# A decoder layer with an interleaved schedule: side work placed by an account of the engines' time, other context products, one conversion on ScalarE, y's split earlier, LayerNorm's buffers locked apart

## The chip, the cores and the metric

The program runs on one core of a Trainium2 chip. The metric is the time of one execution on the device in microseconds (us). TensorE (PE in the profile) multiplies matrices and loads weights beside it (PEld); VectorE (DVE), ScalarE (ACT) and GpSimd (POOL) work element by element; SyncE (SP) issues DMAs, and so does POOL. Each engine runs its own list of instructions in order and waits on semaphores for the others.

## The reference, cut to what matters

A batch of 16 sequences of 256 tokens of width 512 goes through one decoder layer: x plus a Mamba-2 mixer, plus a linear cross attention on a context, plus a gated feed-forward network (FFN) with quantised weights and activations.

```python
x = x + _L0_attn_ref(_layernorm(x), ...)                       # Mamba-2, 32 heads of 64, state 64
x = x + _L0_xattn_ref(_layernorm(x), ctx_1024, ctx_1024, ...)  # 16 heads of 32
x = x + _L0_ffn_ref(_layernorm(x), w_gate, w_up, w_down)       # 2048 inner, weights to -1, 0, 1

# _L0_xattn_ref
qh = sigmoid(q @ wq + bq); kh = sigmoid(k @ wk + bk)
vh = (v @ wv + bv).reshape(b, s, h, dv)
kv = einsum('bsh,bshd->bhd', kh, vh)
state = cumsum(kv, axis=1)
out = einsum('bsh,bhd->bshd', qh, state).reshape(b, s, d) @ wo + bo
```

## The kernel before, in words

**Pairs, slots and units.** Two batches make a pair (k = 0 to 7). The 2048 inner channels of the mixer are cut into 16 units of 128. One unit of one pair is a slot: 128 slots, one after the other, in the loop at line 1927. A slot s works on three units in flight: u0 = s is projected, u1 = s-1 is scanned out and u2 = s-2 goes through the output product. On TensorE a slot is always: six of the 12 products of the z projection (L676), the four transposes of u1's x (`turn_x`, L941), the other six, the 12 products of the x projection (L676, `project_part(u0, 1)`), u1's scan output (`scan_out`, L961 and L968), and u2's output product (L1011, 12 products into four accumulators that stand for a whole pair).

**The other engines in a slot.** VectorE: `times_g` (L929, L933), `scan` (two of L912), then the three convolution taps of u0 (L693, which read the x projection in PSUM after `conv_x`, L897), `plus_dx` (L976) and `gated` (L981), which makes y. ScalarE: eight of L951 (`x_dt`), `silu_z` (L891), the copy yh of y (L987, in `split_y`), `conv_x` (L897), the square of y (L998), `cross` (four of L920) and `silu_x` (L906). POOL: yl = y - yh (L988) and the sum of squares (L999). yh and yl are y's two halves for the output product; each has one buffer, and so has y.

**Side work.** Everything else is written as Python generators that yield what they need next ("dve, 0.7 us"), and `advance(now)` lets them go on at eight points of a slot. POINTS = 8; VectorE's steps may stand at points 1, 2, 5 and 6, ScalarE's at 0, 5 and 6, TensorE's at 3 (just before the scan output, in a turn of the two projection banks, called "z") and at 7 (after the output product, in a bank of its own). What may stand there is decided by `due` (line 1714) from a sum per engine and half slot that has a ceiling (`room`, 2.0 to 4.0 us), and by `Banks.take` (line 297) for PSUM. A step marked "must" (`leaves`) is placed whatever the sum. The side work is: the next pair's LayerNorm (`norm_transposed`, line 607), its time steps (`time_steps`, line 698) and states (`states`, line 777), all started by `plan` three slots before the end of a pair (`c == NU - 3`, for the pair after the next); the end of a batch with its attention queries (`batch_end`, line 1049); the context, two batches at a time (`context_pair`, line 1201), and its groups (`context_group`, line 1298); and the quantising of the FFN's weights (`ffn_quantised`, line 1463) in 48 chunks.

**The FFN** follows in 32 tiles of 128 tokens, 48 products of 128 x 512 each (L1579, L1621).

**Order.** The program's order is written out by hand (`manual_schedule`), so an engine's list is exactly the order in which the Python text calls. A DMA on SP or POOL that waits for data holds up those behind it.

**Locks of the generators.** `Shared` counts a resource in the order of the text. `lns` (one) stands for the normalised tile y ("ln") and its two 16-bit halves ("ln_hi", "ln_lo") together and is held from the load to the transposing DMAs; `turned` (two) for the transposed halves of a pair; `attends` (one) for the attention's tail; `chunks` (three) for weight chunks.

Of the kernel before, what the change touches and what calls it, by code (L numbers as in the profile page):

```python
# [36 lines left out]
F32 = mybir.dt.float32  # L37
# [10 lines left out]
P = 128  # L48
# [10 lines left out]
def decoder_kernel(  # L59
# [135 lines left out]
    with ExitStack() as part:  # L195
# [74 lines left out]

        class Shared:
# [16 lines left out]
        class Banks:  # L288
# [3 lines left out]
            def __init__(self):  # L292
                self.free = {"own": True, "z": True}
                self.line = []
                self.since = 0

            def take(self, own=False, first=False):
                me = [own]
                self.line.insert(0 if first else len(self.line), me)
                while True:  # L300
                    moment = clock[0] % POINTS
                    if steady() and moment == 3:

                        others = [one for one in self.line if not one[0]]
                        if self.free["z"] and others and others[0] is me:
                            hold = "z"
                            break
                    elif self.free["own"] and self.line[0] is me and (
                        not steady() or moment == 7 and clock[0] >= self.since
# [5 lines left out]
                self.free[hold] = False  # L315
                return hold

            def give(self, hold):
                self.free[hold] = True
                if hold == "own":  # L320
                    self.since = clock[0] + 4

        bank = Banks()

        def misc(hold, shape, name):
# [5 lines left out]
        chunks, stages, lns, turned, turned_q, attends, ctxs, outs, xs, late, preps, streams = (  # L331
            Shared(n) for n in (3, 3, 1, 2, 1, 1, 1, 2, 3, 1, 2, 2)
# [274 lines left out]
        def norm_transposed(src, b, what, store):  # L607

            yield from lns.take(rank=0 if what == "m" else 2 if "late" in store else 1)
# [13 lines left out]
            nc.vector.tensor_scalar(rs, mv[:, :, 1], EPS, LN_UP**-2, ALU.add, ALU.mult)  # L623
            hi = p1.tile([P, NT, D], F16, tag="ln_hi", name=f"lnh_{what}_{b}")
# [13 lines left out]
            nc.gpsimd.tensor_tensor(lo, y, hi, ALU.subtract)  # L638
            if what == "q":
                yield from turned_q.take(rank=2 if "late" in store else 1)  # L640
# [14 lines left out]
            lns.give()  # L655
# [42 lines left out]
        def time_steps(pair):  # L698
# [4 lines left out]
            hold = yield from bank.take(first=True)  # L703
# [49 lines left out]
            hold = (yield from bank.take(first=True)) if k else "tp"  # L753
# [23 lines left out]
        def states(pair):  # L777
# [5 lines left out]
            hold = yield from bank.take()  # L783
# [26 lines left out]
            for j in range(2):  # L810
                yield pe(0.4)
                hold = yield from bank.take()
                pg = misc(hold, [P, 3, P], f"pg_{k}_{j}")
                for n, (s0, t0) in enumerate(((0, 0), (P, P), (0, P))):
                    nc.tensor.matmul(
                        pg[:, n, :], bcT[0:NS, j, s0 : s0 + P], cT[:, j, t0 : t0 + P],
                        start=True, stop=True,
# [3 lines left out]
                    g[:, j, 0:2, :], pg[:, 0:2, :], upper.unsqueeze(1).to_broadcast([P, 2, P]),  # L821
# [1265 lines left out]
```

## Time and profile before

| | |
|---|---|
| median of 3 runs | 1882.19 us (1882.07 to 1885.43) |
| the profiled execution, its own time | 1887.88 us |
| its span, first to last instruction | 1886.1 us |
| busy in the span: PE, DVE, ACT, POOL | 95%, 87%, 66%, 36% |
| first slot's scan output to the end of pair 0 | 50.5 to 242.5 us |
| pairs 1 to 7, scan output to scan output | 242.5 to 1525.8 us |
| the rest, FFN above all | 1525.8 to 1886.1 us |

A busy TensorE is not one at its peak, since matmuls are pipelined: the products of 128 x 512 last 383 ns each by their rows but start 0.215 us apart. What counts is the stretch from one slot's start to the next. An engine that is not the last to arrive may idle at no cost.

### The profile page before, as it was taken

The page shows a single profiled execution, that of the slowest core. Times are in us where ns is not written, and L with a number is a line of the kernel's source. Part 1 is how long each engine was busy: PE and PEld are TensorE (multiplying, and loading weights), DVE is VectorE, ACT ScalarE, POOL GpSimd, SP SyncE. Part 2 cuts the span into 40 slices and gives each one's busy share as a digit, 9 for nine tenths or more (in the row PEclk, how much of TensorE's full clock was granted, in tenths as well). Part 3 has the DMA queues.
Part 4 walks back from the last instruction along what each step waited for, and adds up shares of the span by engine and source line. Part 5 has one row for each costly group of instructions (what it writes and reads, how often), then busy time and mean ns, then how long its engine had stood idle before and what let it go on. Part 6 is the DMA issues. An engine that isn't in the chain of part 4 may idle for free.

```text
span 1886.1 us, 30373 instructions
## 1 busy us (share of the span) xinstructions
PE 1786.5 (95%) x10464; PEld 1018.1 (54%) x10464; DVE 1638.2 (87%) x2711; ACT 1248.1 (66%) x2896; POOL 682.2 (36%) x691
## 2 busy tenths in 40 slices
PE   6789999998999998999999999998999989999998
PEld 4445555555556555555555555565656544444443
DVE  6989888777888889888988998989887888999997
ACT  5777666675666666666666666666666557777775
POOL 1233432344434354546454636463533222211000
PEclk8999999999999999999999999999999999999999
DMA  5764776788768777877597879787867734655454
GB/s 163 240 185 136 235 191 174 217 257 223 168 196 270 201 196 235 258 192 191 185 268 211 199 205 252 202 193 186 238 188 213 250 89 99 133 123 130 108 120 95
DMA packets 296933, 358.95 MB, mean 190 GB/s; under 512 B 163765, under 2 KB 197861, under 8 KB 296778
## 3 DMA queue, kind: packets, MB, share of 16 engines
q1 hardware_dynamic: 277962, 296.13, 60.0%
q0 software_dynamic: 18240, 60.84, 9.4%
q8 instruction: 83, 1.36, 0.3%
q14 instruction: 72, 0.59, 0.1%
q10 hardware_dynamic: 576, 0.04, 0.0%
HBM read 279.70 MB, written 39.58 MB: 169 GB/s over the span
## 4 chain that ended last, share of the span: by engine, by line
PE 57%; DVE 25%; DMA 7%; ACT 5%; issue 4%; POOL 2%; SPq 1%; ACTq 0%; POOLq 0%; DVEq 0%
PE pp L676 21%; PE po L1011 11%; PE po_f L1621 5%; PE pg L1579 4%; PE pu L1579 4%; DVE m L912 4%; DVE xs L693 4%; PE py L961 4%; DVE m L929 2%; PE trx L941 2%; DMA w<-w_d 2%; PE py L968 2%; DVE m L933 1%; DVE sp_q L742 1%; DVE y L976 1%
## 5 line engine op out<-in xcount | busy, mean ns | idle before, releaser
L676 PE MATMUL pp<-lnT_h_m,w 128*128 128x512 f16 (+1 forms) x2056 | 661.1, 383 | 23.3 <-DVE xs L693 20.8
L676 PEld LDWEIGHTS <-w 128*128 128x128 f16 x3084 | 296.5, 99 | 364.3 <-issue 35.8
L988 POOL TENSOR_TENSOR yl<-y,yh 128x512 fp32r<-128x512 f32 x128 | 178.9, 1398 | 717.5 <-ACT yh L987 659.3
L693 DVE SCALAR_TENSOR_TENSOR xs<-pp,convw_sb,xs 128x510 f32<-128x510 f32 (+2 forms) x384 | 286.1, 745 | 151.1 <-ACT xs L897 141.6
L676 PE MATMUL pp<-lnT_l_m,w 128*128 128x512 f16 (+1 forms) x1028 | 393.4, 383 | 0.0
L1011 PE MATMUL po<-wout,yh 128*128 128x512 f32 x1024 | 337.0, 410 | 4.6 <-DMA wout<-wout_d 4.6
L951 ACT ACTIVATE xdt<-trx,dt 128x64 f32<-128x64 f32 x1024 | 223.5, 328 | 167.4 <-PE trx L941 167.3
L912 DVE TENSOR_TENSOR_SCAN m<-dab,starts 128x512 f32<-128x512 f32 x254 | 302.2, 1230 | 0.5 <-DMA dab<-da_d 0.5
L1011 PEld LDWEIGHTS po<-wout,yh 128*128 128x128 f32 x1024 | 183.8, 189 | 61.3 <-issue 15.1
L1011 PE MATMUL po<-wout,yl 128*128 128x512 f32 x512 | 203.7, 398 | 3.0 <-POOL yl L988 3.0
L906 ACT ACTIVATE xs<-xs 128x512 f32<-128x512 f32 x128 | 80.9, 632 | 186.3 <-DVE xs L693 186.3
L961 PE MATMUL py<-m,xdt 128*64 128x256 f32 x1024 | 162.1, 395 | 11.1 <-DVE m L933 5.2
L1579 PEld LDWEIGHTS <-yT 128*128 128x128 bf16 x1024 | 100.0, 98 | 131.1 <-issue 14.7
L920 ACT ACTIVATE m<-edb,m 128x128 f32<-128x128 f32 x508 | 162.7, 395 | 12.1 <-DVE m L912 12.1
L999 POOL TENSOR_TENSOR ssq<-ssq,sq 128x512 f32<-128x512 f32 x120 | 158.6, 1321 | 27.9 <-ACT sq L998 27.0
L897 ACT ACTIVATE xs<-pp,convb_sb,convw_sb 128x512 f32<-128x512 f32 x128 | 100.3, 783 | 102.2 <-PE pp L676 102.1
L929 DVE TENSOR_TENSOR m<-m,g 128x1024 f32<-128x1024 f32 x128 | 161.9, 1265 | 0.1
L1579 PE MATMUL pg<-w_ffn,yT 128*128 128x512 bf16 x512 | 132.3, 381 | 4.7 <-ACT h L1583 4.7
L1579 PE MATMUL pu<-w_ffn,yT 128*128 128x512 bf16 x512 | 132.3, 381 | 4.6 <-DVE x L1037 4.6
L1621 PE MATMUL po_f<-w_ffn,hT 128*128 128x512 bf16 x512 | 125.4, 379 | 2.0 <-DMA hT<-hq 2.0
L1583 ACT ACTIVATE h<-pg,sg 128x512 f32<-128x512 f32 x128 | 86.6, 683 | 51.6 <-PE pg L1579 51.3
L1011 PEld LDWEIGHTS po<-wout,yl 128*128 128x128 f32 x512 | 96.7, 189 | 29.7 <-POOL yl L988 6.4
(278 smaller groups left out, 2791.9 us busy)
## 6 DMA issues: line engine op xcount, KB each, us to landing
dab<-da_d SPq DMA_DIRECT2D x127, 512.0 KB
wout<-wout_d SPq DMA_DIRECT2D x112, 512.0 KB
edb<-ed_d SPq DMA_DIRECT2D x127, 256.0 KB
w<-w_d SPq DMA_DIRECT2D x40, 512.0 KB
raw<-in_w_zx SPq DMA_DIRECT2D x16, 512.0 KB
wout_d<-wout SPq DMA_DIRECT2D x16, 512.0 KB
ctxT<-in_ctx_t POOLq DMA_DIRECT2D x16, 512.0 KB, 7.8
x<-in_x SPq DMA_DIRECT2D x16, 512.0 KB
```

Source lines behind the costliest of these rows:

```text
L676: nc.tensor.matmul(dst, w(wi, kc), yT[yi][:, :, kc, :], start=n == 0, stop=n == 3 * KD - 1)
L693: nc.vector.scalar_tensor_tensor(u[:, :, d:S], raw[:, :, 0 : S - d], w[:, j : j + 1], u[:, :, d:S], ALU.mult, ALU.add,)
L912: nc.vector.tensor_tensor_scan(u["m"][:, 4 * j : 4 * j + 4, :].rearrange("p k t -> p (k t)"), u["da"][j].rearrange("p h i t -> p (h i t)") ...
L920: nc.scalar.activation(u["m"][:, 8 + n, :], u["ed"][:, n // 2, n % 2, :], AF.Copy, scale=u["m"][:, 2 * n, P - 1 : P],)
L929: nc.vector.tensor_tensor(m, m, gi.unsqueeze(2).to_broadcast([P, 2, 2, NT * P]), ALU.mult)
L951: nc.scalar.activation(u["xdt"][:, j, i, h, :], u["tr"][:, j, i, h * HD : (h + 1) * HD], AF.Copy, scale=dt[:, i, j, 2 * c + h : 2 * c + h ...
L961: nc.tensor.matmul(py[h * HD : (h + 1) * HD, j, :].rearrange("p (i t) -> p i t", i=NT), xdt[:, j, 0, h, :], m[:, 2 * (2 * j + h) : 9 + 2 * ...
L988: nc.gpsimd.tensor_tensor(lo, u["y"], hi, ALU.subtract)
L999: nc.gpsimd.tensor_tensor(pair["ssq"], pair["ssq"], sq, ALU.add)
L1011: nc.tensor.matmul(pair["po"][n], u["yhl"][yi][:, j, i * P : (i + 1) * P], w[:, wi, :], start=c == 0 and p == 0, stop=c == NU - 1 and p == 2,)
L1579: nc.tensor.matmul(dst, yT[:, kc, :], w_ffn[w + kc][:, cols], start=kc == 0, stop=kc == KD - 1)
L1621: nc.tensor.matmul(u["po"], u["hT", k // (KF // 2)][:, k % (KF // 2), :], w_ffn[2 * KD + k // NF][:, (k % NF) * D : (k % NF + 1) * D], sta ...
```

## The change

1. **An account.** A class `Model` holds a time for each of the four engines. Every function of the slot adds its cost to it in the order of the text, and `due` and `Banks.take` ask it, from slot 18 to the last (`modelled()`), whether a side step fits: for VectorE, whether u0's taps would still end before TensorE's list does, for ScalarE and POOL whether they stay near TensorE's place. A step that was refused gets 0.25 us more slack for each slot that it waits, and 0.5 us for each slot beyond its deadline less five. DMAs wait until TensorE's place in the account has passed the time at which their data is made. The ceilings go on ruling before slot 18.
2. **Context products** (`context_pair`, `states`): the four products that turn the 16 keys (L1246, the 128 x 128 keys as weights) become four with the narrow `pick` as weights in four column groups, and one transpose behind ScalarE's tanh; the four products with `sel` (L1277) become two transposes, since the product with the context now lays its rows out by halves and adds over the two token tiles in PSUM (eight products of 256 columns in place of four of 512). One more PSUM hold for each pair of batches. The three products of g (L815) become two, one of them twice as wide.
3. **bfloat16 by ScalarE**: the last step of a weight chunk, t - MAGIC to bfloat16, goes from POOL (L1480) to ScalarE; one more `issued()` stands ahead of its store.
4. **`split_y`** stands before the slot's first products in the text, and so ahead of `x_dt` and `silu_z` on ScalarE's list; it stood after them.
5. **Locks**: the halves get a lock of their own (`halves`), and `lns` is given back as soon as the low half is computed. Late batches lose their lower rank.
6. `plan` starts a pair's work four slots before the end of a pair, not three, with deadlines.

```diff
+        class Model:
...
+            def op(self, engine, us, *after, port=False):
+                start_ = max([self.t[engine]] + [a + 0.1 for a in after])
+                if port:
+                    for a, b in self.pool[-6:]:
+                        if a <= start_ < b:
+                            start_ = b
+                            break
+                    self.port.append((start_, start_ + us))
+                elif engine == "pool":
+                    for a, b in self.port[-8:]:
+                        if a < start_ < b:
+                            start_ = b
+                            break
+                    self.pool.append((start_, start_ + us))
+                self.t[engine] = start_ + us
+                return start_ + us
...
+            def convolved(self, dve, x_end):
+
+                return max(dve, max(x_end, self.t["act"]) + 0.9) + 2.3
...
+                if e == "dve":
+                    if moment < 3:
+                        taps = self.convolved(t["dve"] + us, t["pe"] + X_US)
+                        end = t["pe"] + X_US + Y_US + OUT_US
...
+                    return taps <= end + slack
...
+        Z_US, X_US, Y_US, OUT_US, G_US, SCAN_US = 3.1, 2.6, 1.5, 2.85, 1.9, 2.45
...
+        def modelled():
+            return (NU + 2) * POINTS <= clock[0] < NP * NU * POINTS
...
@@ states @@
-                for n, (s0, t0) in enumerate(((0, 0), (P, P), (0, P))):
+                for n, (s0, t0, t1) in enumerate(((0, 0, S), (P, P, S))):
                     nc.tensor.matmul(
-                        pg[:, n, :], bcT[0:NS, j, s0 : s0 + P], cT[:, j, t0 : t0 + P],
-                        start=True, stop=True,
+                        pg[:, 2 * n : 2 + n, :].rearrange("p n t -> p (n t)"),
+                        bcT[0:NS, j, s0 : s0 + P], cT[:, j, t0:t1], start=True, stop=True,
                     )
...
@@ context_pair @@
-                    nc.tensor.matmul(
-                        pk[:, k, i, :], kp[:, k, i * P : (i + 1) * P], pick, start=True, stop=True
-                    )
...
+                        pk[r : r + 32], pick, kp[:, k, i * P : (i + 1) * P],
                         start=True, stop=True, tile_position=(0, r),
                     )
+            yield leaves(act(0.3, 2))
+            khT = q1.tile([P, P], F32, tag="khT", name=f"khT_{b}")
+            nc.scalar.activation(khT, pk, AF.Tanh, scale=0.5)
+            bank.give(hold)
+            yield pe(0.2, 2)
+            hold = yield from bank.take(us=0.15)
+            pk = misc(hold, [P, 2, NT, 32], f"pk3_{b}")
+            nc.tensor.transpose(pk.rearrange("p k i h -> p (k i h)"), khT, ident)
...
-            for kc in range(KD):
-                nc.tensor.matmul(
-                    pt[:, kc].rearrange("p q k h -> p (q k h)"), tt[:, kc * P : (kc + 1) * P],
-                    sel.rearrange("p q k h -> p (q k h)"), start=True, stop=True,
-                )
+            for n in range(2):
+                nc.tensor.transpose(pt[:, n * P : (n + 1) * P], tt[:, n], ident)
...
@@ ffn_quantised @@
-                yield pool(1.3)
+                yield act(0.65)
                 q = q2.tile([P, 512], BF16, tag="wq8", name=f"wq8_{k}")
-                nc.gpsimd.tensor_scalar(q, t, -MAGIC, None, ALU.add)
+                nc.scalar.activation(q, t, AF.Copy, bias=-MAGIC)
                 chunks.give()
+                yield issued()
...
@@ due @@
+            if task.engine and task.engine != "dma" and modelled():
+                if task.engine == "pe":
+                    if task.ready > model.t["pe"] + 0.3:
+                        return False
+                    task.pe_us = task.us
+                else:
+                    if not task.must and (
+                        task.ready > model.t[task.engine] + 0.2
+                        or not model.fits(task, now % POINTS, task.us)
+                    ):
+                        return False
+                    task.ready = model.op(task.engine, task.us, task.ready, port=task.port)
+                task.engine = None
+                return True
...
@@ plan @@
-            if (s == 1 or c == NU - 3) and k + ahead < NP:
+            if (s == 1 or c == NU - AHEAD) and k + ahead < NP:
...
@@ the slot @@
             advance(now)
+            if u2:
+                split_y(u2)
             project_part(u0, 0, lambda: turn_x(u1))
             x_dt(u1)
             silu_z(u0)
             advance(now + 1)
-            if u2:
-                split_y(u2)
             advance(now + 2)
```

## The prediction

> **What bounds the kernel now.** I read the page's busy times first, then the busy time of the engines by pair (cut at the slots' first scan output), then the waits, then single slots on the timeline.
>
> ```profile
> PE 1786.5 (95%) x10464; PEld 1018.1 (54%) x10464; DVE 1638.2 (87%) x2711; ACT 1248.1 (66%) x2896; POOL 682.2 (36%) x691
> ```
>
> ```profile
> core 0: us, PE busy (x) PEld busy (x) DVE busy (x) ACT busy (x) POOL busy (x), PEclk, DMA share, GB/s
> 242.50:422.90 180.40, 177.56 (x1100) 105.04 (x1099) 144.22 (x204) 121.90 (x335) 64.32 (x74) 1.00 0.74 211
> 422.90:618.80 195.90, 185.28 (x1194) 111.97 (x1193) 157.40 (x232) 128.34 (x346) 76.80 (x82) 0.97 0.79 219
> 1178.60:1361.90 183.30, 176.70 (x1090) 105.18 (x1089) 166.87 (x241) 121.71 (x312) 89.85 (x81) 0.99 0.77 204
> 1361.90:1525.80 163.90, 161.95 (x950) 97.39 (x949) 139.53 (x196) 102.03 (x286) 51.04 (x43) 1.00 0.72 206
> ```
>
> TensorE sets the pace, with VectorE (166.87 of 183.30 us in pair 6, 91%) close behind; ScalarE has a third of its time free. A slot without side work takes 10.08 us from scan output to scan output (slots 27 to 31, 100, 110). 112 such slots would be 1129 us; pairs 1 to 7 take 1283.3, so 154 us are side work or waits. To part them I took every TensorE instruction's distance to the next one and subtracted the smallest that such a neighbourhood usually has: 85 us belong to side products, 61 us are waits above those of clean slots, the rest is scatter. The 61 us are all that an account could win here: about 28 us in slots 7 to 9 of pairs 2 to 6, 10 in slots 32 and 34, 7 in the second slot of each pair behind `root` and `mixed`, 16 elsewhere.
>
> ```profile
> DVE xs L693 <- ACT xs L897: 141.6, 68, 7.4
> PE pp L676 <- DVE xs L693: 20.8, 13, 3.4
> ```
>
> The second line is the main wait: the next z projection wants the bank that the last tap has still to read. The first says that VectorE idles 2.1 us ahead of its taps in 68 slots, so there is room, but not where the bursts are:
>
> ```profile
> 1268.68 3.37 DVE L912 TENSOR_TENSOR_SCAN m<-dab,starts 128x512 f32<-128x512 f32 x2
> 1271.97 1.25 DVE L735 TENSOR_SCALAR sp_s<-sp_v 128x128 f32<-128x128 f32 x1
> 1275.03 2.30 DVE L693 SCALAR_TENSOR_TENSOR xs<-pp,convw_sb,xs 128x510 f32<-128x510 f32 x3
> 1277.39 0.39 PE L676 MATMUL pp<-lnT_h_m,w 128*128 128x512 f16 x1 [3.44 <-DVE xs L693]
> 1278.50:1281.90 3.40, 3.40 (x12) 1.77 (x11) 3.40 (x5) 3.20 (x11) 0.00 (x0) 0.50 0.60 229
> ```
>
> Slot 104: the time steps' first chain (L735 to L739) takes 3.1 us, with 1.05 of it lost behind POOL, declared as 1.2; the taps end late, TensorE waits 3.44 us, and the granted clock is 0.50 for the next 3.40 us, which costs half of that again. The clock fell so six times in pairs 2 to 6: some 10 of the 61 us. The Trainium skill, "TensorE: Matmul & The Clock Gate", section "What's actually happening", gives an idle window of about 3.4 us as what halves the clock; at 459.3 us it fell behind a wait of only 1.95 us. By the page, only three of the six would go with the waits; by the trace, all.
>
> **The change, part by part.**
>
> *Context products.* Before, one pair of batches spends 0.81 us on L1246 and 1.19 on the products of ptk (the eight sums among them), measured from their start to the next product:
>
> ```profile
> L1246 PEld LDWEIGHTS pk<-pick,kp 128*128 128x128 f32 x64 | 8.3, 191 | 3.7 <-DVE kp L1231 2.8
> L1277 PEld LDWEIGHTS ptk<-sel,ttT 128*128 128x128 f32 x64 | 8.2, 192 | 1.2 <-ACT zs L891 0.5
> L1480 POOL TENSOR_SCALAR wq<-wchunk 128x512 bf16<-128x512 f32 x48 | 77.0, 1604 | 2.9 <-DVE wchunk L1476 2.9
> L1555 ACT ACTIVATE yq<-y 128x512 bf16<-128x512 f32 x32 | 20.1, 629 | 43.2 <-DVE y L1547 43.2
> ```
>
> 64 loads for 8 pairs of batches: each float32 product is two instructions with a load of 191 ns each. After: four narrow products, unknown; at least a quarter of L1264's 1.00 us (same groups, 512 columns), 0.25, at most L1246's 0.81; I take 0.35, nearer the row of the same form. One transpose like L755, 0.20. Two transposes like L941 (four in 0.44) 0.22, and the sums, 0.40. That is 1.17 against 2.00. The context product keeps its columns (eight of 256 for four of 512) but doubles its loads: 1.00 to 1.5, I take 1.00. Gain 0.8 per pair of batches, between -0.1 and 0.9. Six of the eight stand where TensorE is the pace: 5 us. g's products lose two of six loads, nothing to 0.25 us of 0.76; 0.15 times 14 is 2 us. **Together -7 us** (0 to -9). ScalarE's tanh takes the place of VectorE's 0.15 us copy; the extra PSUM hold delays the context by up to a slot, covered by the slots that it has to spare.
>
> *bfloat16 by ScalarE.* POOL loses 48 x 1.5 us. ScalarE gains 48 of the row L1555 (the same operation and shape), 48 x 0.63 = 30 us over pairs 3 to 6, which have some 250 us of free ScalarE. It is hidden by the time in which ScalarE waits for the transposes (167 us ahead of L951); queued behind it are yh and `x_dt`, so without that cover it is up to 0.63 us in a slot, 5 us in all if one in six hits. I take 0. The store (POOL's DMA) goes out up to half a slot later, with the chunk already given back; the last chunk ends at 1362 us now, and the weights that it feeds are read from slot 120 on (1447 us). VectorE wins the 6 us that it lost behind L1480.
>
> *`split_y` first.* On ScalarE yh now starts when y is made and the previous output product has read the old yh, about the slot's start, and ends before the transposes do: free. But yl then falls elsewhere:
>
> ```profile
> 826.30 1.76 POOL L988 TENSOR_TENSOR yl<-y,yh 128x512 fp32r<-128x512 f32 x1 [3.30 <-ACT yh L987]
> 826.86 3.41 DVE L912 TENSOR_TENSOR_SCAN m<-dab,starts 128x512 f32<-128x512 f32 x2
> ...
> 811.91 2.33 DVE L912 TENSOR_TENSOR_SCAN m<-dab,starts 128x512 f32<-128x512 f32 x2
> 814.34 1.27 POOL L988 TENSOR_TENSOR yl<-y,yh 128x512 fp32r<-128x512 f32 x1 [4.05 <-DVE kh L1255]
> 816.12 2.31 DVE L693 SCALAR_TENSOR_TENSOR xs<-pp,convw_sb,xs 128x510 f32<-128x510 f32 x3 [1.80 <-ACT xs L897]
> ```
>
> At 826.30 yl asked in the middle of VectorE's chain, was let in behind L933, and the scans took 3.41 us in place of 2.33: 1.08 us lost. At 814.34 it came behind the scans and cost nothing; the taps run beside it. Now y's copy ends some 0.8 us into the four instructions L929, L933, L912, L912 (4.2 us in a row), so nearly every slot pays. In pairs 1 to 7 the hits of yl come to 34 us now, 12 of them on the slot's own instructions (11 hits, 1.06 each), those of ssq to 26. After: 109 x 1.06 = 116, less 34, less 6 of L1480, less 13 if half of ssq's hits go with the emptier POOL: VectorE is busy 63 us longer, of 178 idle. The skill, "SBUF — State Buffer", section "SBUF: two separate sides", speaks against this step too: whichever of a two-input VectorE instruction and a GpSimd one starts first keeps the shared port for its whole length. By that a hit costs up to yl's own 1.27 us, and 109 of them 138 us; the rows say 1.06.
>
> What TensorE sees of it is read from VectorE's idle time slot by slot: where a slot has less than 1.1 us, the lack adds up to 50 us (some 45 slots, nearly all in pairs 3 to 6). Less the 34 us of hits that vanish and 6 of L1480: **+10 us**. If the hits that vanish were in other slots, only 12 and 6 come off: +32. If the account moves all side work to slots with room: 0.
>
> *The account.* It can win the 61 us less what no placing changes: the 7 behind `root`. It also holds a DMA until its data is due, which is what slot 32 lacked (L1011 waits 4.31 us for a wout load that stands on SP behind eight z_d stores). Against it: in `op` a POOL step delays only VectorE's later calls, and `split_y` is called after `times_g` and `scan`, so the account doesn't see the 1.06 us; and the time steps are still declared as 1.2 and 1.7 us, with 2.0 and 2.6 their clean lengths by the rows. So I take half of the bursts (14), half of slots 32 and 34 (5) and a third of the rest (6): **-25 us** (0 to -45).
>
> *The first 16 slots* keep the ceilings. VectorE is busy 176 of 192 us there and yl's hits are 8 us already; at most 15 x 1.06 - 8 = 8 more. **+3 us**.
>
> *Locks, ranks, the earlier start.* The early `lns` lets a batch's load and statistics go ahead of the other's transposes; no instruction is added, and the two DMAs on SP stay in place. 0. The FFN's 360 us keep their order: 0.
>
> Sum: -7 - 25 + 10 + 3 = -19 us. 1887.88 - 19 = 1868.9 for an execution like the profiled one, which stood 5.7 above the median: **1863 us**. Own range 1845 to 1878 (account -15 to -35, collisions 0 to +16).
>
> **Rivals.**
>
> *The account does all it can* (27%): bursts, slots 32 and 34 and half of the rest go, 28 + 10 + 8 = 46, and side work leaves the slots that yl crowds: -7 - 46 + 0 + 1 = -52, 1830 us. For it: the idle 141.6 us ahead of the taps. Against: the blind spots above.
>
> *VectorE takes over* (17%): yl's place in front makes VectorE the bound of pairs 3 to 6. It decides once VectorE's idle time in a slot falls under the 1.06 us that a hit costs, as in 45 slots now. -7 + 32 + 8 - 10 (the account wins little, being blind to it) = +23, 1905 us. For: 91% busy. Against: pairs 1, 2 and 7 have the room.
>
> *Nothing to be seen* (8%): the account moves the waits and wins 6, collisions and first slots cost 13, products give 7: 0, 1882 us. A measurement of this kernel tells some 0.2% (4 us) from no change.
>
> The forecast has 48%. Range 1828 to 1896: half of the first rival and most of the third stay inside. Faster 0.72, same 0.06, slower 0.22, the forecast's rare misses shared out.
>
> **What would show it.** Yl close behind L981 and a mean of L912 and L933 up by about 0.25 us each or L929's likewise (1.06 per slot in all): collisions. L676's waits on L693 below 12 us, fewer stretches at clock 0.50 in pairs 2 to 6: the account. No 191 ns loads at the old L1246: products. Wrong would be: yl behind the scans after all, VectorE's busy time unchanged, or a main wait on ScalarE.

## The result, and the profile after

| | before | after |
|---|---|---|
| median, 5 runs each | 1883.53 us (1882.07 to 1885.43) | 1913.77 us (1902.13 to 1916.27) |
| ratio, 95% interval | | 1.0141 [1.0110, 1.0172] |
| profiled execution, its span | 1887.88, 1886.1 us | 1902.13, 1900.4 us |

The changed kernel is slower by 1.4% (the ratio; the medians lie 30.2 us apart); 1863 us was predicted. Its profiled execution is the fastest of its five and the one of before lies 4.4 us above its median, so the traces show 14.3 us more span, and the other 16 us between the medians are in no trace. Three executions on record stand far outside (5334.58 us in e5 below, 2035.04 and 4930.04 us of the kernel before); the ratios leave them out.

The page's busy times of the changed kernel:

```profile
PE 1778.3 (94%) x10456; PEld 1009.0 (53%) x10456; DVE 1686.0 (89%) x2717; ACT 1275.6 (67%) x2944; POOL 656.1 (35%) x642
```

TensorE has less to do (by 8.2 us of modelled time) and takes longer: it waits more. VectorE is busy 48 us longer. The windows of pairs 1, 2, 6 and 7, cut as before at the slots' first scan output:

```profile
core 0: us, PE busy (x) PEld busy (x) DVE busy (x) ACT busy (x) POOL busy (x), PEclk, DMA share, GB/s
247.80:437.60 189.80, 177.64 (x1101) 104.20 (x1100) 160.02 (x208) 125.35 (x345) 77.28 (x81) 0.98 0.74 213
437.60:626.20 188.60, 181.28 (x1193) 108.18 (x1192) 166.29 (x249) 128.17 (x342) 85.38 (x80) 0.99 0.77 220
1195.90:1375.80 179.90, 174.20 (x1083) 103.93 (x1082) 166.23 (x221) 116.47 (x303) 66.27 (x53) 1.00 0.67 189
1375.80:1542.30 166.50, 161.76 (x947) 96.56 (x946) 149.45 (x193) 102.85 (x285) 56.65 (x40) 1.00 0.69 202
```

Against before, pair 1 is 9.4 us longer, pair 2 7.3 shorter, pair 6 3.4 shorter and pair 7 2.6 longer; pairs 3 to 5 between them are 9.9 longer. VectorE is 8.9 us busier in pair 2, which became shorter: that isn't the picture of one engine that has become the bound. The groups that belong to the early split:

```profile
L1030 DVE TENSOR_TENSOR_SCAN m<-dab,starts 128x512 f32<-128x512 f32 x254 | 347.9, 1409 | 0.0
L1116 POOL TENSOR_TENSOR yl<-y,yh 128x512 fp32r<-128x512 f32 x128 | 209.7, 1638 | 519.9 <-ACT yh L1115 458.2 <-PE trx L1063 13.3 <-PE pp L788 12.8
...
L1049 DVE TENSOR_TENSOR m<-m,g 128x1024 f32<-128x1024 f32 x128 | 157.6, 1231 | 0.1
...
L1053 DVE TENSOR_TENSOR m<-m,g 128x512 f32<-128x512 f32 x128 | 123.7, 967 | 0.0
```

Before:

```profile
L912 DVE TENSOR_TENSOR_SCAN m<-dab,starts 128x512 f32<-128x512 f32 x254 | 302.2, 1230 | 0.5 <-DMA dab<-da_d 0.5
L929 DVE TENSOR_TENSOR m<-m,g 128x1024 f32<-128x1024 f32 x128 | 161.9, 1265 | 0.1
L933 DVE TENSOR_TENSOR m<-m,g 128x512 f32<-128x512 f32 x128 | 92.7, 724 | 0.0
```

Together that is 72.4 us less. The work is the same; the surplus fits yl, whose hits on this chain rose from 12 us to 85.1. The waits of TensorE, after and, in the last two lines, before:

```profile
PE py L1086 <- DVE m L1053: 13.7, 8, 5.6
PE pp L788 <- DVE xs L805: 13.4, 8, 2.9
PE pp L788 <- DMA w<-w_d: 10.2, 3, 7.9
PE py L1086 <- ACT xdt L1075: 9.1, 6, 2.8
...
PE py L961 <- DVE m L933: 5.2, 6, 1.1
PE py L961 <- ACT xdt L951: 5.0, 4, 2.1
```

The wait for the taps, which the account looks at, fell from 20.8 us to 13.4 (L788 is the old L676, L805 the old L693). Above and below it stand waits that the account has no number for: the scan output's for `m`, 5.2 us before, its wait for `x_dt`, 5.0 before, and one for a weight stream. In slot 30 and in slot 49 (timeline; the last three lines are the kernel before's):

```profile
399.94 4.76 SPq L1534 DMA_DIRECT2D z_d<-zl  x4
405.26 0.66 SPq L521 DMA_DIRECT2D w<-w_d  x1
419.01 0.61 PE L788 MATMUL pp<-lnT_h_m,w 128*128 128x512 f16 x1 [7.88 <-DMA w<-w_d]
...
639.67 0.81 SPq L1268 DMA_DIRECT2D x_d<-x  x1
645.42 0.38 SPq L1179 DMA_DIRECT2D x<-in_x  x1
650.05 1.41 DVE L1169 SCALAR_TENSOR_TENSOR x<-po,rq,x 128x512 f32<-128x512 f32 x2 [4.85 <-DMA x<-in_x]
651.38 1.21 DVE L1049 TENSOR_TENSOR m<-m,g 128x1024 f32<-128x1024 f32 x1
652.51 0.68 DVE L1053 TENSOR_TENSOR m<-m,g 128x512 f32<-128x512 f32 x1
653.25 1.12 PE L1086 MATMUL py<-m,xdt 128*64 128x256 f32 x4 [5.63 <-DVE m L1053]
...
605.84 0.46 SPq L1135 DMA_DIRECT2D x_d<-x  x1
612.55 0.39 SPq L1046 DMA_DIRECT2D x<-in_x  x1
636.68 2.73 DVE L1037 SCALAR_TENSOR_TENSOR x<-po,rq,x 128x512 f32<-128x512 f32 x4 [1.13 <-POOL rq L1029]
```

In slot 30 the load of the projection's weights w goes out at 405.26, behind four stores of z_d on SP's list, and TensorE waits 7.88 us for it. Before, the same load went out at 395.76, ahead of these stores, and no product waited for it; there the stores held up a load of wout, for which TensorE waited 4.31 us (the slot 32 of the prediction). That wait is gone, and a longer one has come in its place.

Slot 49 reads from the top: a store of x goes out at 639.67 and, 5.75 us behind it, the load of the next x at 645.42. `mixed` (L1169) waits 4.85 us for that load on VectorE, `times_g` stands behind it, and TensorE gets its `m` 5.63 us late. Before, the same store and load stood at 605.84 and 612.55, and `mixed` came at 636.68, 24 us behind the load's issue, and no one waited for it. These two waits are 13.5 us.

My own sums over the records of each trace say where the 14.3 us are (us; "gaps" is TensorE's idle time above 0.1 us in slots 16 to 127, "half" the length of the stretches there at a granted clock of 0.50, of which at most half is lost):

| | first slot to slot 16 | slots 16 to 127 | rest | gaps | half |
|---|---|---|---|---|---|
| before | 192.0 | 1283.2 | 360.4 | 41.5 | 20.5 |
| after | 197.2 | 1294.5 | 358.1 | 59.5 | 27.3 |

5.2 + 11.3 - 2.3 is 14.2. Of the 11.3, gaps are +18.0; the side products' own time, each from its start to the next product's less the gap, is -8.0 (109.4 to 101.4), and that of the slots' own products +1.2 (1131.5 to 1132.7), which together close the sum. The clock hardly shows: 20.3 us of the half-clock stretches lay on the slots' own products before and 21.9 after, and the rest of the 27.3 us after in gaps. By what TensorE did next, the gaps ahead of scan outputs went from 5.5 to 17.0 us and ahead of side products from 5.4 to 14.0, while those ahead of projections stayed (22.2 and 24.0).

### The profile page after: what moved, and what is told of

The parts are those of the page before. It is cut to its first block, busy times and chain, and to the rows that moved or that the text cites. A ratio compares the mean times of both kernels' runs of the same rounds, so it can differ in the third digit from the quotient of the medians.

```text
span 1900.4 us, 30193 instructions
## 1 busy us (share of the span) xinstructions
PE 1778.3 (94%) x10456; PEld 1009.0 (53%) x10456; DVE 1686.0 (89%) x2717; ACT 1275.6 (67%) x2944; POOL 656.1 (35%) x642
## 4 chain that ended last, share of the span: by engine, by line
PE 56%; DVE 25%; DMA 7%; ACT 5%; issue 4%; POOL 1%; SPq 1%; ACTq 0%; DVEq 0%; POOLq 0%
PE pp L788 21%; PE po L1141 10%; PE pg L1714 5%; PE po_f L1756 5%; PE pu L1714 5%; DVE xs L805 4%; DVE m L1030 4%; PE py L1086 4%; DVE m L1049 2%; PE trx L1063 2%; PE py L1093 2%; DVE m L1053 2%; DVE y L1102 1%; DVE y L1108 1%; DMA w<-w_d 1%
## 5 line engine op out<-in xcount | busy, mean ns | idle before, releaser
L788 PE MATMUL pp<-lnT_h_m,w 128*128 128x512 f16 (+1 forms) x2056 | 660.4, 383 | 25.7 <-DVE xs L805 13.4
L788 PEld LDWEIGHTS <-w 128*128 128x128 f16 x3084 | 295.9, 99 | 364.4 <-issue 34.6
L805 DVE SCALAR_TENSOR_TENSOR xs<-pp,convw_sb,xs 128x510 f32<-128x510 f32 (+2 forms) x384 | 286.1, 745 | 123.1 <-ACT xs L1012 113.6
L788 PE MATMUL pp<-lnT_l_m,w 128*128 128x512 f16 (+1 forms) x1028 | 392.7, 382 | 0.0
L1116 POOL TENSOR_TENSOR yl<-y,yh 128x512 fp32r<-128x512 f32 x128 | 209.7, 1638 | 519.9 <-ACT yh L1115 458.2
L1030 DVE TENSOR_TENSOR_SCAN m<-dab,starts 128x512 f32<-128x512 f32 x254 | 347.9, 1409 | 0.0
L1086 PE MATMUL py<-m,xdt 128*64 128x256 f32 x1024 | 163.9, 398 | 23.9 <-DVE m L1053 13.7
L1049 DVE TENSOR_TENSOR m<-m,g 128x1024 f32<-128x1024 f32 x128 | 157.6, 1231 | 0.1
L1053 DVE TENSOR_TENSOR m<-m,g 128x512 f32<-128x512 f32 x128 | 123.7, 967 | 0.0
```

What stands on the lines that cost most here:

```text
L788: nc.tensor.matmul(dst, w(wi, kc), yT[yi][:, :, kc, :], start=n == 0, stop=n == 3 * KD - 1)
L805: nc.vector.scalar_tensor_tensor(u[:, :, d:S], raw[:, :, 0 : S - d], w[:, j : j + 1], u[:, :, d:S], ALU.mult, ALU.add,)
L1030: nc.vector.tensor_tensor_scan(u["m"][:, 4 * j : 4 * j + 4, :].rearrange("p k t -> p (k t)"), u["da"][j].rearrange("p h i t -> p (h i t)") ...
L1049: nc.vector.tensor_tensor(m, m, gi.unsqueeze(2).to_broadcast([P, 2, 2, NT * P]), ALU.mult)
L1053: nc.vector.tensor_tensor(m, m, g[:, :, 2, :].unsqueeze(2).to_broadcast([P, 2, 2, P]), ALU.mult)
L1086: nc.tensor.matmul(py[h * HD : (h + 1) * HD, j, :].rearrange("p (i t) -> p i t", i=NT), xdt[:, j, 0, h, :], m[:, 2 * (2 * j + h) : 9 + 2 * ...
```

## The experiments

Eighteen kernels ran, in five groups; those of a group shared a chip and the runs of the kernel before, and every ratio is to those. The first two theories were: the collisions of the early split cost the time (1), or the account itself does (2).

**The split and the account, two by two.**

```diff
@@ e1_split_late, in the changed kernel @@
-            if u2:
-                split_y(u2)
             project_part(u0, 0, lambda: turn_x(u1))
...
             advance(now + 1)
+            if u2:
+                split_y(u2)
```

> The changed kernel with y's split put back behind silu_z in each slot, all else as changed. Theory 1, collisions (yl in front stops VectorE's scans: 80 hits and 85 us on the slot's chain against 12 hits and 12 us before, in pairs that VectorE already fills): yl's hits on the chain fall below 25, VectorE's busy time falls by 30 to 60 us, and the time falls from 1914 to 1875 to 1895. Theory 2, the account (it delays side work until something on the main path waits for it, whatever POOL does): the hits fall the same, but the time stays within 8 us of 1914.

Measured: 1935.55 us, 1.0253 [1.0229, 1.0276]. The collisions went (yl's hits on `times_g` and the scans fell from 80 to 18, their cost to VectorE from 85.1 to 19.5 us) and the time still rose by 22 us. So taking the collisions away doesn't bring the time back, and neither theory's range holds 1935.55. It doesn't show that they cost nothing in the changed kernel, since the account places the side work anew in e1. TensorE's waits:

```profile
PE pp L788 <- DMA w<-w_d: 13.3, 2, 9.6
PE trx L1063 <- ACT xs L1023: 11.1, 8, 3.5
PE stp L1492 <- ACT zs L1005: 9.5, 1, 9.5
PE py L1086 <- DVE m L1053: 9.5, 6, 1.9
...
PE pa L1255 <- DMA z<-z_d: 8.0, 1, 8.0
```

A weight stream, a state product and the attention's output stand there with 8 to 13 us each in one or two places: loads and side products whose operands came late. Gaps are 86.3 us, the half clock 58.0.

```diff
@@ e2_account_off, in the changed kernel @@
         def modelled():
-            return (NU + 2) * POINTS <= clock[0] < NP * NU * POINTS
+            return False
```

> The changed kernel with the account never asked (the ceilings of before rule all slots), all else as changed, the early split of y included. Theory 1: the collisions stay (over 70 hits) and so does the time, 1905 to 1935, since the account can only have helped. Theory 2: the waits behind late side work (a late load of x, 5.7 us; a late weight stream, 8 us) go, and the time falls to 1880 to 1898.

Measured: 1936.30 us, 1.0272 [1.0250, 1.0295]. Without its account the changed kernel is slower still, so theory 2 falls in this form. The waits for the taps are 25.3 us now, and the new transpose waits for its tanh:

```profile
PE pp L788 <- DVE xs L805: 25.3, 18, 3.9
PE trx L1063 <- ACT xs L1023: 13.2, 10, 2.8
PE pk L1384 <- ACT khT L1379: 12.7, 3, 6.3
```

e9 has both edits, of e1 and of e2.

> The changed kernel with the account never asked and y's split behind silu_z: new products, bfloat16 by ScalarE and locks alone. The fourth corner beside the changed kernel (1914), the account alone off (1936) and the split alone late (1936). If split and account only add up, late costs 22 us here too: 1950 to 1965. If the early split is bad by its collisions and good only because of how the account places side work, late is better without the account, as it is without all else (15 us): 1912 to 1928.

Measured: 1917.34 us, 1.0172 [1.0140, 1.0204]. The four corners are 1.0141 (account, early split), 1.0272 (early alone), 1.0253 (account alone) and 1.0172 (neither). The effects don't add: the account wins 25 us with the early split and costs 15 with the late one; the early split wins 21 with the account and costs 19 without. Neither part has a price of its own here. TensorE's gaps go much the same way: 59.5, 81.9, 86.3 and 69.7 us.

**The split alone**, in the kernel before: the lines of e1's edit the other way round.

> The kernel before with y's split put first in the slot, nothing else. Theory 1: VectorE loses 60 to 90 us more behind yl and the time rises by 15 to 35 us, to 1898 to 1918. Theory 2: VectorE has the room, the time stays within 6 us of 1883.

Measured: 1899.88 us, 1.0077 [1.0057, 1.0097], some 15 us and as theory 1 said (here and below a price is the ratio less one, times the time of before beside it), where my terms for it were +10 and +3. Its scans:

```profile
L912 DVE TENSOR_TENSOR_SCAN m<-dab,starts 128x512 f32<-128x512 f32 x254 | 371.7, 1503 | 0.0
```

yl hits the chain 96 times in pairs 1 to 7 and costs VectorE 107.6 us; 109 and 116 were foretold.

**The products.** e4 puts the new context products and g's products (item 2 of the change, without the account's arguments) into the kernel before.

> The kernel before with the new context products and the two products of g, nothing else. Both theories: TensorE's side products fall by some 0.8 us per pair of batches and little at g, 5 to 9 us in all, and the time falls by as much, to 1874 to 1880, unless the one more PSUM hold moves other side work to worse places (then up to 1890).

Measured: 1922.51 us, 1.0194 [1.0168, 1.0221]: +37 us from a part that I had at -7, the largest miss of the study. One of the places, on ScalarE and TensorE:

```profile
459.94 0.63 ACT L906 ACTIVATE xs<-xs 128x512 f32<-128x512 f32 x1 [3.58 <-DVE xs L693]
460.48 1.50 ACT L632 ACTIVATE ln_m<-ln_m,ln_mv_m,ln_rs_m 128x512 f32<-128x512 f32 x2
462.02 1.05 ACT L636 CAST lnh_m<-ln_m 128x1024 f16<-128x1024 f32 x1
462.97 0.27 ACT L1246 ACTIVATE khT<-pk 128x128 f32<-128x128 f32 x1
...
463.29 0.47 PE L1251 MATMUL pk<-ident,khT 128*128 128x128 f32 x1 [5.34 <-ACT khT L1246]
```

The tanh of 0.27 us stands in ScalarE's order behind `silu_x` and two steps of a LayerNorm; the transpose that needs it stands in TensorE's order ahead of everything else, and 5.34 us pass. This wait is 8.2 us in three places; a load of the time steps' input (6.5 us, once) and 31 us at half clock more (51.2) came with it. Five kernels took the part to pieces.

```diff
@@ e5_same_steps: the products with no new step (g, ptt, ptk); keys as before @@
-                for n, (s0, t0) in enumerate(((0, 0), (P, P), (0, P))):
+                for n, (s0, t0, t1) in enumerate(((0, 0, S), (P, P, S))):
...
-            for kc in range(KD):
-                nc.tensor.matmul(
-                    pt[:, kc].rearrange("p q k h -> p (q k h)"), tt[:, kc * P : (kc + 1) * P],
...
+            for n in range(2):
+                nc.tensor.transpose(pt[:, n * P : (n + 1) * P], tt[:, n], ident)
```

> The kernel before with the part of the new context products that needs no new step (the products with the context laid out by halves, two transposes in place of the four with sel, g in two products); the key product and every wait, PSUM hold and declared time of the generators as before, so that all other instructions keep their places. Theory A (the products are right and what costs in the 1922 us of the products alone is the one more step): the time falls by 4 to 8 us, to 1877 to 1881. Theory B (the new instructions themselves cost, in TensorE or in the longer chain of copies): 1890 or more.

Measured: 1885.14 us beside 1886.29, 0.9991 [0.9980, 1.0002]. Between the two theories: harmless, and by the interval worth at most 4 us.

```diff
@@ e6_empty_hold: in the kernel before, one more hold that nothing uses @@
-            yield dve(0.1)
+            yield pe(0.2, 2)
+            hold = yield from bank.take()
+            yield leaves(dve(0.1))
+            bank.give(hold)
```

> The kernel before with one more, empty PSUM hold in each pair of contexts, where the new products have the transpose of the keys: no instruction is added or taken away, only the places of the side work move. Theory A: if it is the shift of places alone that costs, most of the 37 us, so 1905 to 1925; if it is the transpose's own wait for ScalarE's tanh, within 8 us of 1885. Theory B: within 8 us of 1885.

Measured: 1903.41 us, 1.0080 [1.0054, 1.0107]. Not one instruction differs in kind, size or number from the kernel before, only the order of the side work (the hold, and the VectorE step behind it, which is placed as "must" now), and 15 us are lost, a little less than theory A said. The profiled execution, 1893.54 us, is the second fastest of six; its gaps are 44.9 us and its half clock 27.3, against 41.5 and 20.5, so its trace shows only 5.7 of the 15.

```diff
@@ e7_transpose_later: e4, and @@
-            yield pe(0.2, 2)
+            yield pe(0.2, 4)
```

> The kernel with the new products alone, but the transpose of the keys may come four points after the tanh in place of two, so that it is not put in the same slot's end. If the transpose's wait for ScalarE (8.2 us in 3 waits there) and the half clock behind it are the cause, L1251 waits under 1 us and the time falls from 1922 to 1895 to 1910; if it is the shift of places, it stays between 1910 and 1930.

Measured: 1898.77 us, 1.0066 [1.0051, 1.0082], 24 us less than e4. The time lies where the theory of the tanh had it, but the transpose still waits, now for something else that ScalarE does (first line; the other two are e4's):

```profile
PE pk L1251 <- ACT zs L891: 4.3, 1, 4.3
...
PE pk L1251 <- ACT khT L1246: 8.2, 3, 5.3
PE pk L1251 <- ACT zs L891: 2.8, 1, 2.8
```

So its own waits fell from 11.0 to 4.3 us, 6.7 of the 24. TensorE's gaps fell from 71.8 to 52.0 in all, most of that elsewhere, and the half clock did not go with the tanh's wait (51.2 and 54.6).

e8 is the changed kernel with the old context and g products.

> The changed kernel with the old context products and the three products of g; account, bfloat16 by ScalarE, early split and locks as changed. If the products cost 37 us here too, 1870 to 1885; if the account keeps the added step away from bad places, the time is 1905 to 1925, near the changed kernel's 1914.

Measured: 1901.81 us, 1.0088 [1.0071, 1.0105]. Beside 1.0141 the new products cost the changed kernel about 10 us too; 1901.81 lies between the two ranges.

e12 is the changed kernel with e7's edit.

> The changed kernel with the transpose of the keys four points behind the tanh in place of two. With ceilings this won 24 us. If the account already keeps the transpose away from a late tanh (no wait of the transpose for khT stands among the longest there), it moves by less than 8 us, 1906 to 1921; if the products' cost of 12 us in the changed kernel is this wait, 1895 to 1905.

Measured: 1894.47 us, 1.0037 [1.0024, 1.0051], the best with the account. But the changed kernel's transpose had no wait for its tanh to lose: what fell were gaps ahead of projections (24.0 to 12.3 us) and of scan outputs (17.0 to 9.8), while those ahead of side products rose (14.0 to 19.5). It is another shift of places and not e7's mechanism.

**The rest.** e10 is the kernel before with bfloat16 on ScalarE, the locks and the earlier start.

> The kernel before with bfloat16 by ScalarE, the locks and ranks and the start four slots before the end of a pair: no account, split late, old products. If these are the harmless part: 1880 to 1895. If they move side work to bad places as the products do: 1900 to 1930.

Measured: 1908.38 us, 1.0107 [1.0082, 1.0131]. +20 us from three parts that I had at nothing. One by one (e14 takes the ranks with the locks; e15 lets the conversion follow after one point, without the added `issued()`, where e10 has four points and `issued()`):

```diff
@@ e14_locks_alone @@
-            yield from lns.take(rank=0 if what == "m" else 2 if "late" in store else 1)
+            rank = 0 if what == "m" else 1
+            yield from lns.take(rank=rank)
...
+            yield from halves.take(rank=rank)
             hi = p1.tile([P, NT, D], F16, tag="ln_hi", name=f"lnh_{what}_{b}")
...
             nc.gpsimd.tensor_tensor(lo, y, hi, ALU.subtract)
+            lns.give()
...
-            lns.give()
+            halves.give()
@@ e15_act8_alone @@
-                yield pool(1.3)
+                yield act(0.65, 1)
                 q = q2.tile([P, 512], BF16, tag="wq8", name=f"wq8_{k}")
-                nc.gpsimd.tensor_scalar(q, t, -MAGIC, None, ALU.add)
+                nc.scalar.activation(q, t, AF.Copy, bias=-MAGIC)
@@ e16_start_earlier @@
-            if (s == 1 or c == NU - 3) and k + ahead < NP:
+            if (s == 1 or c == NU - 4) and k + ahead < NP:
```

> The kernel before with the locks of LayerNorm's tile and halves parted and the ranks of late batches gone, nothing else. No instruction differs. If any shift of places costs, 1895 to 1910; if locks are free, within 6 us of 1886.

> The kernel before with the 48 conversions to bfloat16 by ScalarE (without the added pause ahead of the store). ScalarE gets 30 us more, POOL loses 72, VectorE is freed of 6 us. If the instructions count: 1878 to 1886. If the shift of places counts (the step may stand at other points): 1890 to 1910.

> The kernel before with a pair's LayerNorm, time steps and states started four slots before the end of a pair in place of three. No instruction differs. If any shift of places costs: 1890 to 1910; if an earlier start only gives slack: 1880 to 1888.

Measured: the locks and ranks 1898.34 us, 1.0055 [1.0036, 1.0075]; bfloat16 on ScalarE 1885.21, 0.9988 [0.9974, 1.0002]; the earlier start 1888.14, 1.0003 [0.9990, 1.0016]. The last two are free, as predicted. The locks and ranks, which again change no instruction, cost 10 us by order alone. The other 10 of e10's 20 us belong to none of the three by itself; whether they come of the three together or of the longer pause around the conversion wasn't tried.

**The account alone**, e13: the class, its calls in the slot, `due` and `Banks.take` as in the changed kernel; everything else as before.

> The kernel before with the account alone deciding where side work stands: old products, split late, bfloat16 by GpSimd, old locks, start three slots before a pair's end. Theory account (it places well and the other parts spoil it): 1850 to 1878. Theory late work (what it refuses is waited for later, by side products, loads and weight streams): 1895 to 1925, with fewer waits for taps and more of side products.

Measured: 1913.12 us, 1.0128 [1.0105, 1.0152], +24 us. Its waits show what it does and what it doesn't:

```profile
PE po L1138 <- POOL yl L1113: 11.8, 7, 7.3
PE trx L1060 <- ACT xs L1020: 11.8, 9, 1.9
...
PE py L1083 <- DVE m L1050: 8.7, 5, 3.2
PE py L1083 <- ACT xdt L1072: 7.6, 4, 3.4
...
PE pp L785 <- DVE xs L802: 2.3, 4, 1.1
```

The wait that it was made for fell from 20.8 us to 2.3, better than I had given it. But TensorE now waits for yl (3.0 us before), for ScalarE ahead of the transposes (6.0 before) and at the scan output. Gaps went from 41.5 to 57.1 us, the half clock from 20.5 to 47.8.

```diff
@@ e11_account_told: the changed kernel; the scans' price in the account knows of yl @@
-                u["t_m"] = model.op("dve", 1.22, port=True)
+                u["t_m"] = model.op("dve", 1.22 + 0.7 * j, port=True)
```

> The changed kernel with an account that is told of 0.7 of the 1.06 us that yl costs the scans in a slot. Theory blind account (it fills slots that the collision has already filled): waits for taps and scan out fall, 1885 to 1905. Theory late work (what it refuses comes later and is waited for): side work gets later, waits of side products, loads and streams grow, 1915 to 1945.

Measured: 1915.62 us, 1.0145 [1.0120, 1.0170], no different from the change. The blind spot that I had named, closed by two thirds, gave nothing: the gaps ahead of side products grew to 30.5 us. The full 1.06 us wasn't tried.

**What is left when the harmful parts go.** e17 is e5 and e15 together; e18 adds the time steps' clean lengths:

```diff
@@ e18_true_lengths: e17, and in time_steps @@
-            yield dve(1.2)
+            yield dve(2.0)
...
-            yield dve(1.7)
+            yield dve(2.6)
```

> The kernel before with the context products that need no new step and the conversions to bfloat16 by ScalarE. Alone they gave ratios of 0.9991 and 0.9988, neither clear of 1. If these are real and add up: 1880 to 1885 beside 1887.7, ratio 0.996 to 0.999. If placing decides, anything within 10 us of 1888.

> The same with VectorE's two chains of the time steps declared as 2.0 and 2.6 us, as long as their instructions last, in place of 1.2 and 1.7. If the ceilings then keep other VectorE work out of their half slots, the waits of slots 7 to 9 fall by half and the time by 8 to 14 us, 1870 to 1878; if side work is only pushed to other slots, 1885 to 1900.

Measured: e17 1885.54 us, 0.9985 [0.9969, 1.0001]; e18 1884.23, 0.9986 [0.9973, 1.0000], beside 1887.55. Neither is clearly faster than the kernel before. In e18 the bursts had more room declared, and the wait for the taps was 25.8 us, not less than e17's 24.4. No version tried is clearly faster than the kernel before.

## Why the prediction was wrong, by its own steps

**The step under all terms.** Each term was priced by its own instructions or its own wait, with all other side work left in its place. That is the step that failed: an edit that moves the order and no instruction costs 15 us (e6) or 10 (e14), and two parts that move it together don't add (the four corners). How the 30 us of the changed kernel divide among its parts stays open.

**"Together -7 us" (products).** The instructions were sized about right: per pair of batches 2.00 us of TensorE became 1.06 (1.17 foretold; the four narrow products 0.36 for my 0.35, the transpose 0.11 to 0.20 by what follows it, the context product 1.00 as taken, ptk's group 0.59), and the side products of pairs 1 to 7 gave 8.0 us, 1.0 of it because one context product now stands ahead of slot 16. What failed here is the half sentence "the extra PSUM hold delays the context by up to a slot, covered by the slots that it has to spare". Time to spare is about the context's due time; it says nothing on where the other side work goes when the context's steps move. e6 prices that alone at 15 us and e4 the whole part at 37, 8.2 of it a transpose's waits for a tanh. I had weighed the tanh by its length against VectorE's copy, not by its place in ScalarE's order.

**"-25 us" (the account).** Alone it costs 24 us (e13); in the changed kernel it wins 25 (e2). That this is the size of my term is luck, since the sign turns with the place of the split. I priced it by the waits of before, as if removing a wait that it counts made no other. The sign I looked for ("L676's waits on L693 below 12 us, fewer stretches at clock 0.50 in pairs 2 to 6") came in e13 for the waits (2.3) and not in the changed kernel: 13.4 us, and the stretches in pairs 2 to 6 add up to 20.5 us as before. Slots 7 to 9 of these pairs did gain: their time above 10.08 us a slot, less their side products, fell from 29.0 to 14.8 us. What took its place I hadn't costed: the waits for loads, for yl, for `x_dt` and for the operands of side products. The price against it that I did name, blindness to 1.06 us per slot, wasn't what mattered as far as e11 shows, which told the account of 0.7.

**"+10" and "+3" (split first).** Right in mechanism, and alone in size: 96 hits and 15 us of time (e3). In the changed kernel the hits came too, 72 of 1.06 us in pairs 1 to 7 for my 109 (8 more in pair 0), and VectorE was busy 48 us longer for my 63; but there the late split is 21 us worse (e1), so as terms of this sum +10 and +3 had the wrong sign. The half of ssq's hits that I guessed would vanish did (26 to 13.6 us). The 80 hits cost 85.1 us by the trace. By the rule of the Trainium skill, "SBUF — State Buffer", section "SBUF: two separate sides", a hit could cost up to yl's own 1.27 us, an estimate of 102 us for the 80, and the trace lies below it. One reading was off: the taps at 816.12 start after yl, which ends at 815.61, so that row doesn't show the two side by side; 28 other taps of the trace of before do run beside yl and last 747 ns, the rest 745.

**"0" (bfloat16 on ScalarE, earlier start).** Right (e15, e16): 48 instructions cost ScalarE 28.1 us (28.9 in the changed kernel) and the time nothing, and no VectorE instruction waits behind L1480 any more, since it isn't on POOL.

**"0" (locks, ranks).** Wrong by 10 us (e14). I counted instructions and DMAs, of which none changed, and not the order.

**The rivals.** "The account does all it can" fell with its premise. "VectorE takes over" foretold 1905 us and came nearest, but its reason isn't borne out: with the collisions taken out (e1) the time was worse. The case that the runs speak for, that each part reshuffles the side work of a schedule whose waits depend on its places, had no chance of its own. The bounds of the own range, added up from the brackets beside it, are 1843 and 1879 and not 1845 and 1878; nothing hangs on it.

**Open.** Why the account and the early split help each other and harm alone isn't settled. e13's waits for yl point to it, but e1, which has the account and the late split, shows no such wait among its large ones. What the changed kernel's other four executions lost beyond the profiled one (8 to 14 us) is in no trace, but their mean granted clock is on record: 0.979 to 0.981 against 0.985. Over 1912 us that is an estimate of 8 to 12 us, so the clock alone could account for most of it; which waits brought it down isn't known.

## What to carry to other kernels

In a schedule written out by hand and already tuned, an edit has two prices: its instructions, and the order that it gives to everything placed after it. Measure the second with an empty edit (a hold that nothing uses, a lock that only splits); if that alone moves the time by 10 to 15 us, a gain of 7 us in instructions can't be predicted by sizing them, and parts must be tried together. A placer that counts one wait can move the loss to those that it doesn't count (e13): expect the waits to turn up there. Whether one that also counts loads and the delay of each operand's engine would do better wasn't tried.

## What the runs showed of the hardware that was not expected

The granted clock adds to small waits. In the stretch of slot 104 before (1278.50 to 1281.90 us, at 0.50) the projection's products start 0.43 us apart, and 0.21 us apart behind it. Through the eighteen kernels the stretches at 0.50 in slots 16 to 127 add up to between 13.7 us (e18) and 58.0 (e1), so up to 7 and up to 29 us are lost to it beside the waits themselves. In the changed kernel a single stretch follows slot 49 (window):

```profile
651.20:658.00 6.80, 4.75 (x21) 3.28 (x22) 6.73 (x9) 1.65 (x5) 0.00 (x0) 0.50 0.33 92
```

It begins 3.6 us into TensorE's wait of 5.63 and lasts 4.75 us beyond it; in the kernel before one of 3.40 us followed a wait of 3.44. The six such stretches of pairs 2 to 6 before stand behind waits of 4.31, 1.95, 3.26, 3.09, 1.57 and 3.44 us: two of the six, and not the prediction's three, are 3.4 us or more, and two are under 2 us. The scatter of one program goes with the clock too. Ninety executions of the kernel before, beside the experiments, go from 1879.37 to 1894.74 us: the 12 with a mean granted clock of 0.983 have a median of 1889.9 us, the 14 with 0.987 one of 1882.8. e6's two with 0.987 took 1893.33 and 1893.54 us, and its other four, with 0.979 to 0.984, 1900.66 to 1907.42.
